# Order of the transfers behind an attention unit, and of three small steps at the start, in a two-layer kernel on one core

## The chip, the cores and the metric

The kernel runs on one core of one Trainium2 chip, in float32. A core has TensorE (PE), VectorE (DVE), ScalarE (ACT), GpSimd (POOL) and SyncE (SP), each with its own instruction stream, and 16 DMA engines that serve transfers issued by SP, ACT and POOL. The metric is the device time of one execution in microseconds (us), as the median of several runs.

## The reference

There are 8 sequences of 128 rows with 512 features. The first layer multiplies each sequence by an adapter matrix chosen by its number (`w0`, 8 matrices of 512x512) and sends the result through a base matrix with eight low-rank experts, of which the top two count. The second layer is attention with a paged cache, then a feed-forward part with 64 small experts. Cut to what matters:

```python
w = weight[adapter_ids];  c = einsum('bsi,boi->bso', x, w)     # adapter matrix by number
x = x + experts(c)                                              # base + top-2 low-rank experts
q, k, v = x Wq, x Wk, x Wv                                      # 32 query heads, 8 key heads, D = 128
q, k = rope(rmsnorm(q)), rope(rmsnorm(k))                       # tables of cos and sin by position
kc, vc = k_cache[block_table], v_cache[block_table]             # 16 pages of 32 rows a sequence
p = softmax(mask([q kc, q k] * SCALE));  o = p [vc; v];  y = o Wo
x = x + ffn(x + y)                                              # 64 experts of rank 8, top 16
```

## The kernel before

**The first layer** is a loop over the 8 sequences (`t`). `l0_load(b)` (L503 to L508) fetches a sequence's `xT` and its adapter matrix (1 MB): SP reads the number from `ids` into a register (`value_load`, L505) and issues the DMAs. For the first sequence the matrix comes in three pieces (256, 256 and 512 KB), all on SP's queue, and PE's first products `cp` (L626) take the pieces one after the other. Until they come PE runs products on an identity matrix whose result nobody uses (L730). Further on in a step, DVE does the routing of the experts (L653 to L671, the last is `low`), PE transposes `low` (`ltp`, L683), and DVE makes the new `x` (L691). Besides, `l0_rows` (L567 to L571) works out, from the page table `vpg`, the row numbers `vrow` by which POOL later gathers value pages, and `l0_angles` (L594 to L607) works out angles for the tables. Both are DVE work put into chosen steps of the loop by hand.

**The attention** is a list of 64 units. A turn `st` is one sequence with one pair of key heads; there are 32 turns, each of two units `u` (`GH = 2`). `iteration(u)` is one pass of a software pipeline written out by hand; its parts work on different units:

- `scores(u, h)` for the four query heads of unit u on PE: against the cached keys `kt` (L439) and the new ones (L442). They need `kt` of the turn and `qkT` of the unit. `mask_exp` follows on DVE (L452) and ACT (L463), `normalize` on DVE and POOL (L468, L469).
- `blocks` (L474) and `blocks_qk` (L425) on DVE transpose 32x32 blocks of the probabilities and of the queries and keys of unit u+2 into `pb`, of which there is one buffer.
- `exchange_out(u)` writes `pb` to DRAM (`px`) in four DMAs of 400 KB, two issued by SP and two by ACT (L486).
- `exchange_in(u - 1)` reads it back in another order: `qkb` (320 KB, queries and keys of unit u+1, L933), then `pT` (1280 KB, probabilities, L936), both issued by SP. `heads_qk` (ACT, L943) copies `qkb` into `qkT`, which the scores of the next unit take. `values(u - 2)` on PE multiplies `pT` with the values (L956).
- `gather` (L193) fetches key pages of the next turn, eight in each unit, 32 KB each: SP reads the page's number into a register and issues the DMA. Five stand ahead of `exchange_in`, three behind it. `gather_v` (L203) on POOL fetches the value pages.
- `make_tables` (L236, POOL) multiplies the norms' weights with cos and sin for a turn, three units ahead.
- `output(u - 3, h)` issues PE's products with the output matrix (`y`, L1081), a head at a time behind the scores of that head; DVE adds them up (L1150, L1168). `project` (L262) makes queries, keys and values for later turns, in blocks of products with sums ahead and behind.

All engines run what was issued in program order. SP's order in a unit is five key pages, `qkb`, `pT`, three key pages, then `px` of the unit:

```python
            if pages:
                gather(st + 1, first, first + 5)
            if on(u - 1):
                exchange_in(u - 1)
            if pages:
                gather(st + 1, first + 5, end)
```

After the last unit PE still has the feed-forward part's tail (L1445).

Of the kernel before, what the change touches and what calls it, by code (L numbers as in the profile page):

```python
# [58 lines left out]
def adaln_ffn_kernel(  # L59
# [374 lines left out]
    def scores(u, h, which=None):  # L434
        st, g = units[u]
        kt, _ = kv_t[st]
        qkT = qkT_t[u]
        s = banks(f"s_{u}_{h}", which)
        nc.tensor.matmul(  # L439
            out=s[:, :L], lhsT=qkT[:, h, :], rhs=kt[:, :, g % GH, :], start=True, stop=True  # L440
        )
        nc.tensor.matmul(  # L442
            out=s[:, L:NK], lhsT=qkT[:, h, :], rhs=qkT[:, REP, :], start=True, stop=True
        )
        s_t[u, h] = s
# [20 lines left out]
    def normalize(u, h):  # L466
        den = den_t.pop((u, h))
        nc.vector.reciprocal(den, den)  # L468
        nc.gpsimd.tensor_scalar(p_t[u, h], p_t[u, h], den, 1.0, ALU.mult, ALU.mult)  # L469
# [23 lines left out]
    with ExitStack() as l0:  # L493
# [6 lines left out]
        def l0_load(b):  # L500
            xT = p2.tile([P, NC, S], F32, tag="xT", name=f"xT_{b}", bufs=3)
            eng = nc.scalar if b == 0 else nc.sync
            eng.dma_start(out=xT.rearrange("p c n -> p (c n)"), in_=xt[b])  # L503
            wt = wt_home.pop(b)
            a = nc.sync.value_load(ids[0:1, b : b + 1])  # L505
            at = (0, P, 2 * P, DM) if b == 0 else (0, DM)
            for n, end in zip(at, at[1:]):
                nc.sync.dma_start(  # L508
                    out=wt.rearrange("p o n -> p (o n)")[:, NC * n : NC * end],
                    in_=w0[ds(a, 1), :, NC * n : NC * end].rearrange("e p n -> p (e n)"),  # L510
                )
            loaded[b] = [xT, wt]

# [77 lines left out]
        def l0_angles(part):  # L591

            if part == 0:
                nc.vector.tensor_copy(lenf, leni)  # L594
                pos = w0p.tile([P, B], F32, name="pos")
                nc.vector.tensor_scalar(pos, lenf, pf, None, ALU.add)
                nc.vector.tensor_tensor(
                    ang,
                    pos.unsqueeze(2).to_broadcast([P, B, D // 2]),
                    fr.unsqueeze(1).to_broadcast([P, B, D // 2]),  # L600
                    ALU.mult,
                )
                nc.vector.tensor_scalar(kk, ang, INV_2PI, ROUND, ALU.mult, ALU.add)
                nc.vector.tensor_scalar(kk, kk, ROUND, None, ALU.subtract)
            elif part == 1:
                for c in (C1, C2, C3):
                    nc.vector.scalar_tensor_tensor(ang, kk, -c, ang, ALU.mult, ALU.add)  # L607
            elif part == 2:
                nc.vector.tensor_scalar(ang, ang, PI_LOW, -PI_LOW, ALU.min, ALU.max)
                nc.vector.scalar_tensor_tensor(kk, ang, -1.0, ang, ALU.mult, ALU.max)  # L610
            else:
                nc.scalar.activation(sin, ang, AF.Sin)
                nc.scalar.activation(cos, kk, AF.Sin, bias=half_pi, scale=-1.0)
# [117 lines left out]
        for t in range(B):  # L731
            l0_adapter(t, True)
            if t >= 1:
                l0_turn_low(t - 1)
            if t == 7:
                scores(0, 1, 1)
                mask_exp(0, 1)
                normalize(0, 0)
            l0_adapter(t, False)
            if t == 0:  # L740
                l0_fold()
            if t + 3 < B:
                l0_load(t + 3)
            if t + 2 < B:
                l0_load_x(t + 2)
            if t in (3, 4):
                load_q(t - 3)
            if 2 <= t <= 5:
                gather(0, (t - 2) * 4, (t - 1) * 4)
            elif t > 5:  # L750
                gather(1, (t - 6) * 8, (t - 5) * 8)
            if t >= 2:
                l0_turn(t - 2)
            if t == 4:
                project_whole(0, 0, 0, 1)
            if t == 5:
                norms(0)
                make_mask(0)
                project_whole(0, 1, 0, 1)
            if t == 6:  # L760
                transpose_qk(0)
                project_whole(0, 0, 1, 1)
            if t == 7:
                make_tables(2)
                norms(2)
                project_whole(0, 1, 1, 1)
                transpose_qk(1)
            if t >= 1:
                l0_experts(t - 1)
            if t == 7:  # L770
                scores(0, 2, 1)
                mask_exp(0, 2)
                normalize(0, 1)
                new_pb(0)
                blocks(0, 0)
            l0_base(t)
            if t == 0:
                l0_small()
            if t == 1:
                l0_rows()  # L780
                nc.vector.tensor_scalar_mul(nw[:, 0, :], nw[:, 0, :], -SCALE)
            if 1 <= t <= 4:
                l0_angles(t - 1)
            if t in (3, 6):
                gather_v(t // 3 - 1, 0, LC)
            if t in (4, 5):
                make_tables(t - 4)
            if t == 4:
                project_whole(0, 0, 0, 0)
            if t == 5:  # L790
                project_whole(0, 1, 0, 0)
                norms(1)
                rotate(0)
                sums_q(nc.gpsimd, 0, 3, 2)
            if t == 6:
                scores(0, 0, 1)
                mask_exp(0, 0)
                project_whole(0, 0, 1, 0)
                rotate(1)
                sums_q(nc.gpsimd, 0, 4)  # L800
            if t == 7:
                scores(0, 3, 1)
                mask_exp(0, 3)
                normalize(0, 2)
                blocks(0, 1)
                project_whole(0, 1, 1, 0, "kv")
# [118 lines left out]
    with ExitStack() as l1:  # L925
# [1 line left out]
        wk2 = l1.enter_context(tc.tile_pool(name="l1_2", bufs=2))  # L927

        def exchange_in(u):
            m = px_t.pop(u).rearrange("k b i f -> (k b) i f")  # L930
            if u + 2 in range(4, NU):
                qkb = wk1.tile([P, QD, NH * 32], F32, tag="qkb", name=f"qkb_{u + 2}")
                nc.sync.dma_start(out=qkb, in_=m[:, :, PW:])  # L933
                qkb_t[u + 2] = qkb
            pT = wk1.tile([P, QD, PW], F32, tag=f"pT{u % 2}", name=f"pT_{u}")
            nc.sync.dma_start(out=pT, in_=m[:, :, :PW])  # L936
            pT_t[u] = pT
# [325 lines left out]
        def iteration(u):  # L1263
# [23 lines left out]
                exchange_in(u - 1)  # L1287
            if pages:
                gather(st + 1, first + 5, end)
            if pages:  # L1290
                gather_v(st + 1, u % GH * LC // GH, (u % GH + 1) * LC // GH)
            if on(u + 3) and u % GH == 1 and u > 1:
                make_tables(units[u + 3][0])
            if on(u - 3) and u % 4 == 3 and (u - 3) // 4 < WHOLE_PAIRS:
                load_y((u - 3) // 4)
# [15 lines left out]
                norms(u + 3)  # L1311
            for h in range(REP):
                if on(u):
                    if (u, h) not in ((1, 0), (1, 1), (2, 0)):
                        scores(u, h)
                        mask_exp(u, h)
                    if h > 0 and (u, h) != (1, 1):
                        normalize(u, h - 1)

                    if (u, h) == (1, 2):  # L1320
                        transpose_qk(3)

                    sums_o(u, h)
                    sums_w(u, h)
                    if 16 <= u < NU - 8 and (r, h) == (2, 3):
                        load_o(u // 16, (1, B12))

                    if h == 2:
                        new_pb(u)
                        if u + 2 in range(4, NU):  # L1330
                            blocks_qk(u + 2, u)
                    if h > 1:
                        blocks(u, h - 2)
                    if h == 1 and u == NU - 5:
                        f_fold()
                    if h == 3:
                        z_blocks(u - NU + 4)
                    if h == (1 if u == NU - 3 else 2) and fb is not None:
                        yT_t[fb] = f_turn(fb, *f)
                if on(u - 3):  # L1340
                    output(u - 3, h)
                    sums_a(u - 3, h)
                if h > 0 and slots:
                    project(k, j, slots[h - 1 : h])

                if (u, h) in WHOLE:
                    project_whole(1, *WHOLE[u, h])
# [12 lines left out]
                f_weights(u - NU + 7)  # L1360
            if on(u):
                normalize(u, REP - 1)
            if 3 < u < NU - 3:
                norms(u + 3)
            if u == 1:
# [192 lines left out]
```

## Time and profile before

| | |
|---|---|
| time, three runs | 1205.39, 1205.78, 1211.27 us; median 1205.78 |
| profiled execution | 1209.55 us, its span 1207.8 us, granted TensorE clock 1.0 |
| PE, DVE, POOL, ACT busy | 99%, 76%, 61%, 42% of the span |
| moved by DMA | 302 MB, 250 GB/s in the mean |
| DMA queues (share of 16 engines) | SP's q1 53.2%, ACT's q10 13.6%, POOL's q0 12.4% |
| one unit of the attention | 16.24 us from px issue to px issue (mean, units 5 to 57) |

In the groups, a row gives line, engine, operation, output and inputs by the program's names with shapes, the number of instructions, busy time and the mean of one in ns, and then the idle time of the engine just ahead of them with what ended it. In the chain of waits a row is the start, the length, and what the time went to, followed back from the last instruction.

### The profile page before, as it was taken

To read this page: it belongs to the slowest core of one execution; us is meant where nothing else is said; L and a number is where in the kernel's file an instruction comes from. 1 tells how busy PE (TensorE), PEld (TensorE's weight loads), DVE (VectorE), ACT (ScalarE), POOL (GpSimd) and SP (SyncE) were. 2 spreads that over 40 slices of the span, in tenths; PEclk is the share of its full clock that TensorE was granted. 3 is DMA by queue.
4 is the path that set the end of the run, shared out by engine and by line. 5 is a ranking of instruction groups with operands and counts; after the bars stand their busy time and mean duration, and the time that the engine had idled before them with its cause. 6 is when DMAs were issued, how large, how long until landed. Compare 5 with 4: busy or idle time off the path is not lost.

```text
span 1207.8 us, 16783 instructions
## 1 busy us (share of the span) xinstructions
PE 1194.7 (99%) x4156; PEld 714.6 (59%) x4156; DVE 913.1 (76%) x2103; ACT 504.3 (42%) x1457; POOL 740.4 (61%) x828
## 2 busy tenths in 40 slices
PE   9999999999999999999999999999999999999998
PEld 7666545565555556555556555555656555555554
DVE  2647788787888787878887887879887888787632
ACT  1345534443444444444444444444444444443211
POOL 3545769778755686578647685687657784643100
PEclk9999999999999999999999999999999999999999
DMA  8823777888888988888789978887989888898742
GB/s 315 287 89 113 247 238 245 263 265 264 264 253 257 301 244 278 260 287 282 237 258 282 294 240 281 285 289 246 279 255 302 254 263 251 261 281 230 232 140 97
DMA packets 205300, 302.31 MB, mean 250 GB/s; under 512 B 84755, under 2 KB 119316, under 8 KB 204180
## 3 DMA queue, kind: packets, MB, share of 16 engines
q1 hardware_dynamic: 170308, 196.81, 53.2%
q10 hardware_dynamic: 18576, 52.04, 13.6%
q0 software_dynamic: 16320, 52.40, 12.4%
q8 instruction: 33, 0.54, 0.2%
q14 instruction: 63, 0.52, 0.1%
HBM read 185.44 MB, written 115.74 MB: 249 GB/s over the span
## 4 chain that ended last, share of the span: by engine, by line
PE 82%; DMA 6%; POOL 4%; DVE 3%; issue 2%; SPq 1%; ACT 1%; ACTq 0%; DVEq 0%; POOLq 0%
PE o L956 18%; PE p L262 18%; PE s L439 16%; PE y L1081 13%; PE s L442 4%; PE p L295 3%; DMA px<-pb 2%; PE op L1445 2%; PE y L1094 2%; PE bp L648 1%; PE cp L626 1%; DMA kt<-in_kc 1%; PE fr L866 1%; POOL p L469 1%; DVE pb L474 1%
## 5 line engine op out<-in xcount | busy, mean ns | idle before, releaser
L463 ACT ACTIVATE p<-p,low 128x640 f32<-128x640 f32 x256 | 211.8, 828 | 433.7 <-DVE den L468 267.4
L469 POOL TENSOR_SCALAR p<-p,den 128x640 f32<-128x640 f32 x256 | 210.2, 822 | 233.4 <-DVE den L468 232.5
L452 DVE CUSTOM_DVE_ANT_0 p<-s,mask,rs 128x640 f32<-128x640 f32 x256 | 222.3, 878 | 81.6 <-PE s L442 80.7
L262 PE MATMUL p<-wqkv,xo 128*128 128x384 f32 x784 | 281.1, 487 | 0.7 <-DVE c L265 0.3
L439 PE MATMUL s<-kt,qkT 128*128 128x512 f32 x504 | 258.7, 595 | 4.5 <-DMA kt<-in_kc 2.6
L956 PE MATMUL o<-pT,vt 128*128 128x512 f32 x512 | 230.2, 592 | 0.0
L474 DVE STREAM_TRANSPOSE pb<-p 128x640 f32<-128x640 f32 x248 | 204.8, 826 | 25.6 <-POOL p L469 25.5
L1081 PE MATMUL y<-wo,oT 128*128 128x256 f32 x784 | 206.6, 380 | 0.9 <-DVE yp L1168 0.5
L262 PEld LDWEIGHTS p<-wqkv,xo 128*128 128x128 f32 x784 | 148.2, 190 | 70.2 <-POOL wqkv L163 1.6
L442 PEld LDWEIGHTS s<-qkT 128*128 128x128 f32 x504 | 95.8, 190 | 120.5 <-issue 120.5
L203 POOL DMA_INDIRECT vt<-in_vc,vrow x128 | 137.6, 1075 | 40.8 <-issue 31.9
L956 PEld LDWEIGHTS o<-pT,vt 128*128 128x128 f32 x512 | 97.2, 190 | 107.8 <-issue 92.8
L439 PEld LDWEIGHTS s<-kt,qkT 128*128 128x128 f32 x504 | 94.2, 190 | 78.3 <-issue 32.5
L1081 PEld LDWEIGHTS y<-wo,oT 128*128 128x128 f32 x784 | 131.9, 191 | 9.8 <-PE s L442 1.2
L311 ACT ACTIVATE sq<-c 128x128 f32<-128x128 f32 x320 | 98.8, 309 | 9.5 <-DVE oT L474 1.4
L442 PE MATMUL s<-qkT 128*128 128x128 f32 x504 | 96.8, 274 | 0.0
L317 POOL TENSOR_TENSOR rs<-ss,mhalf 128x5 f32<-128x5 f32 x64 | 82.2, 1284 | 5.3
L979 ACT COPY oT<-o 128x512 f32<-128x512 f32 x64 | 37.4, 585 | 102.3 <-PE o L956 77.2
L315 POOL TENSOR_SCALAR ss<-ss,eps 128x5 f32<-128x5 f32 x64 | 27.6, 431 | 74.3 <-ACT sq L311 74.3
L956 PE MATMUL o<-pT,vn 128*128 128x512 f32 x128 | 65.4, 592 | 0.0
L425 DVE STREAM_TRANSPOSE pb<-ca 128x640 f32<-128x640 f32 x60 | 50.2, 836 | 18.1 <-DMA px<-pb 8.2
L265 DVE TENSOR_TENSOR c<-c,p 128x384 f32<-128x384 f32 x84 | 44.9, 534 | 22.9 <-PE p L262 22.7
(198 smaller groups left out, 1441.3 us busy)
## 6 DMA issues: line engine op xcount, KB each, us to landing
pT<-px SPq DMA_DIRECT2D x64, 1280.0 KB, 6.6
px<-pb SPq DMA_DIRECT2D x120, 400.0 KB, 5.2
px<-pb ACTq DMA_DIRECT2D x120, 400.0 KB, 4.2
qkb<-px SPq DMA_DIRECT2D x60, 320.0 KB, 3.4
kt<-in_kc SPq DMA_DIRECT2D x512, 32.0 KB, 5.1
wqkv<-in_wqkv POOLq DMA_DIRECT2D x32, 384.0 KB, 4.8
wo<-in_wo POOLq DMA_DIRECT2D x17, 512.0 KB, 7.5
yd<-yp POOLq DMA_DIRECT2D x12, 512.0 KB, 9.0
```

What stands on the lines that cost most here:

```text
L203: nc.gpsimd.indirect_dma_start(out=kv_t[step][1][:, c, :], out_offset=None, in_=vc, in_offset=bass.IndirectOffsetOnAxis(ap=vrow[:, hf, at ...
L262: nc.tensor.matmul(out=ps, lhsT=xo[:, pr, x, c, :], rhs=w[:, c, :], start=(c == 0), stop=(c == 1))
L311: nc.scalar.activation(sq, cs[:, at : at + D], AF.Square, accum_out=ss[:, h : h + 1])
L317: nc.gpsimd.tensor_tensor(rs, ss, mhalf, ALU.pow)
L439: nc.tensor.matmul(out=s[:, :L], lhsT=qkT[:, h, :], rhs=kt[:, :, g % GH, :], start=True, stop=True)
L442: nc.tensor.matmul(out=s[:, L:NK], lhsT=qkT[:, h, :], rhs=qkT[:, REP, :], start=True, stop=True)
L452: nc.vector.tensor_tensor_reduce(out=p, in0=s_t.pop((u, h))[:, :NK], in1=mask_t[st], scale=rs_t[u][:, h : h + 1], scalar=BIG, op0=ALU.add, ...
L463: nc.scalar.activation(p, p, AF.Exp, bias=low, scale=-1.0, accum_out=den)
L469: nc.gpsimd.tensor_scalar(p_t[u, h], p_t[u, h], den, 1.0, ALU.mult, ALU.mult)
L474: nc.vector.transpose(pb_t[u][:, :, h * w : (h + 1) * w].rearrange("p i (j a) -> p j i a", a=32), p_t.pop((u, h)).rearrange("p (j i a) -> ...
L956: nc.tensor.matmul(out=o, lhsT=vt[:, c, j * D : (j + 1) * D] if c < LC else vn_t.pop(u), rhs=pT[:, c], start=(c == 0), stop=(c == LC),)
L1081: nc.tensor.matmul(out=y_t["y"][:, half * HN : (half + 1) * HN], lhsT=part(key)[:, i * S : (i + 1) * S], rhs=wo_t[:, slot(w, key[0] // (B ...
```

## The change

Five places change.

1. The first adapter matrix is fetched in four pieces of 256 KB, issued by SP and ACT in turns. Both engines read the adapter's number into a register of their own.
2. `l0_rows` and the scaling of `nw` move from step 1, ahead of that step's angles, to step 2, behind its angles.
3. `exchange_in` issues only `qkb`. The read of `pT` becomes a function of its own, `probs_in`, called behind the last three key pages of the unit. SP's order becomes five pages, `qkb`, three pages, `pT`, `px`.
4. The tables of turn 3 are made at the end of unit 2, behind its last `normalize`, where unit 3 made them behind its gathers.
5. From unit 5 on, in each fourth unit (u % 4 == 1), the scores of query heads 0 and 1 are both issued ahead of the output products of head 0; before, the scores of head 1 stood behind them.

```diff
@@ l0_load
-            a = nc.sync.value_load(ids[0:1, b : b + 1])
-            at = (0, P, 2 * P, DM) if b == 0 else (0, DM)
-            for n, end in zip(at, at[1:]):
-                nc.sync.dma_start(
+            both = (nc.sync, nc.scalar) if b == 0 else (nc.sync,)
+            which = [e.value_load(ids[0:1, b : b + 1]) for e in both]
+            at = range(0, DM + 1, P if b == 0 else DM)
+            for i, (n, end) in enumerate(zip(at, at[1:])):
+                both[i % len(both)].dma_start(
                     out=wt.rearrange("p o n -> p (o n)")[:, NC * n : NC * end],
-                    in_=w0[ds(a, 1), :, NC * n : NC * end].rearrange("e p n -> p (e n)"),
+                    in_=w0[ds(which[i % len(both)], 1), :, NC * n : NC * end].rearrange("e p n -> p (e n)"),
                 )
@@ first layer, step t
-            if t == 1:
+            if 1 <= t <= 4:
+                l0_angles(t - 1)
+            if t == 2:
                 l0_rows()
                 nc.vector.tensor_scalar_mul(nw[:, 0, :], nw[:, 0, :], -SCALE)
-            if 1 <= t <= 4:
-                l0_angles(t - 1)
@@ exchange_in
-            m = px_t.pop(u).rearrange("k b i f -> (k b) i f")
+            m = px_t[u].rearrange("k b i f -> (k b) i f")
...
+        def probs_in(u):
+            m = px_t.pop(u).rearrange("k b i f -> (k b) i f")
             pT = wk1.tile([P, QD, PW], F32, tag=f"pT{u % 2}", name=f"pT_{u}")
             nc.sync.dma_start(out=pT, in_=m[:, :, :PW])
@@ iteration
                 gather(st + 1, first + 5, end)
+            if on(u - 1):
+                probs_in(u - 1)
             if pages:
                 gather_v(st + 1, u % GH * LC // GH, (u % GH + 1) * LC // GH)
-            if on(u + 3) and u % GH == 1 and u > 1:
+            if on(u + 3) and u % GH == 1 and u > 3:
                 make_tables(units[u + 3][0])
...
-                    if (u, h) not in ((1, 0), (1, 1), (2, 0)):
-                        scores(u, h)
-                        mask_exp(u, h)
+                    ahead = u > 1 and u % 4 == 1
+                    for n in (((0, 1), (), (2,), (3,)) if ahead else ((0,), (1,), (2,), (3,)))[h]:
+                        if (u, n) not in ((1, 0), (1, 1), (2, 0)):
+                            scores(u, n)
+                            mask_exp(u, n)
...
                 normalize(u, REP - 1)
+            if u == 2:
+                make_tables(3)
```

## The prediction

> **What bounds the kernel now.** First the busy table of the page and its row of slices:
>
> ```profile
> PE 1194.7 (99%) x4156; PEld 714.6 (59%) x4156; DVE 913.1 (76%) x2103; ACT 504.3 (42%) x1457; POOL 740.4 (61%) x828
> DMA  8823777888888988888789978887989888898742
> ```
>
> TensorE (PE) is busy for 99% of 1207.8 us. The change takes no matmul away, so all it can give is time in which PE waits. I measured that from the trace's matmul starts: each gap between two starts, less the usual pitch of a matmul of that width (0.84 ns a column). The pitches sum to 1179.0, the gaps to 23.9, the rest is the first start (1.4) and the tail (3.6). These 23.9 us are the pool for any gain; a loss has no such limit. The second row says what else is full: the 16 DMA engines are 0.7 to 0.9 busy from start to end.
>
> Second, the PE groups with what ended the idle time before them, over the span and (last line) over the first 45 us:
>
> ```profile
> L439 PE MATMUL s<-kt,qkT 128*128 128x512 f32 x504 | 258.7, 595 | 4.5 <-DMA kt<-in_kc 2.6 <-ACT oT L979 0.7 <-PE o L956 0.6
> L1081 PE MATMUL y<-wo,oT 128*128 128x256 f32 x784 | 206.6, 380 | 0.9 <-DVE yp L1168 0.5 <-DVE yp L1150 0.4
> L626 PE MATMUL cp<-xT,wqkv 128*128 128x128 f32 x128 | 15.9, 277 | 1.3 <-DMA wqkv<-in_w 1.2
> ...
> L683 PE MATMUL ltp<-ident,low 128*128 128x128 f32 x3 | 0.9, 292 | 0.9 <-DVE low L671 0.9
> ```
>
> These are four of the change's five places: scores that wait for key pages, output products that wait for an addition on VectorE (DVE), the first adapter products that wait for their matrix, and a transpose at 38 us that waits for DVE.
>
> Third, the chain of waits (start, length, what) for the places where DMA sets the pace:
>
> ```profile
> 3.73 5.76 DMA wqkv<-in_w
> ...
> 144.67 5.57 DMA px<-pb
> 156.76 5.78 DMA kt<-in_kc
> ...
> 552.96 7.72 DMA px<-pb
> 567.90 8.62 DMA px<-pb
> 580.70 5.18 DMA kt<-in_kc
> ```
>
> Twice px (the probabilities on their way out) is on the chain as well as the pages: DMA is close behind PE.
>
> **Part 1, first adapter matrix.** In the timeline SP issues the three pieces at 2.62, 3.20 and 3.73 (256, 256, 512 KB). PE starts at 6.03, gaps of 0.26 and 1.37 follow, and the last `cp_0` product ends near 11.5. After: pieces 0 and 2 on SP, 1 and 3 on ACT, which must first read the adapter number (0.47 on SP at 1.94). The pieces share 16 engines that were 0.7 to 0.95 busy under one queue between 3 and 8 us. So two pieces land together, the first later (I estimate 6.4 to 6.9 against 5.9), the last at 8 to 9 against 9.45, as the last 512 KB are cut in two and issued sooner. `cp_0` then ends between 10 and 12. Bounds -1.4 to +0.5 us; I take -0.8, nearer to the gain because the 1.37 gap is the larger one and the last piece ends it. ACT's two issues (some 0.35 each by SP's rows) lie in its wait for the first copy at 11.63; its table load (1.28, from 1.15) is pushed back and still ends by 5. From 12.5 to 37 PE has no gap, so the gain is passed on.
>
> The Trainium skill speaks against this part: its page "DMA: Bandwidth & Descriptors", section "Issuing engines are not separate DMA queues", says that DMAs of different issuers run on the same 16 engines and that a second issuer saves only the time to start one, usually small. By it the gain would be the issue times alone (0.34 and less), with the first piece later: about nothing.
>
> **Part 2, row numbers.** DVE sits at L568 from 27.08 to 30.24 for the page table (`vpg`); then come the rows (0.8), the scaling of `nw` (0.2), and the angles (1.6), so that `x_1` (L691) starts at 33.16, 2 us after its PSUM bank was ready. The routing chain behind ends with `low` at 38.13, and PE waits 1.07 for it. Moved behind the next angles, the wait is over long before; DVE comes 2 us earlier, which is more than 1.07. In its new place the 1.1 us fall into DVE's wait for the third `x` (40.2 to 41.6); without that cover they would cost 1.1. `vrow` has its first reader one step later. -1.07.
>
> **Part 3, key pages ahead of the probabilities.** In each unit SP waits for px, issues qkb (320 KB), pT (1280 KB), then the three last pages. The three pages go into the queue behind 1.28 MB. The scores of each even unit need them:
>
> ```profile
> 577.27 0.54 SPq L933 DMA_DIRECT2D qkb<-px  x1
> 577.86 0.62 SPq L936 DMA_DIRECT2D pT<-px  x1
> 579.01 2.02 SPq L193 DMA_DIRECT2D kt<-in_kc  x3
> ```
>
> In this unit (30) the last page is issued at about 580.7 and lands 5.18 later (the chain above); PE starts the scores 1.21 late. The same kind of gap stands at units 4 (1.76), 14 (0.38), 18 (0.83), 24 (0.17) and 58 (0.59): 4.9 in all. After, the pages are issued 0.6 us sooner and behind 320 KB instead of 1600; pT's packets take about 4 us, so they land 4 to 5 us sooner, and none of these gaps is over 1.8. Next after the pages is `qkT` (ACT L943, ready 1.4 to 7 us before the scores), whose qkb read keeps its place. -4.9, bounds -4.9 to -2.5 (if `qkT` or the mask takes half).
>
> What it delays is pT. Mean over units 2 to 59: px issue to its last packet 8.06, then 0.94 to qkb's issue, then 7.25 to pT's last packet: 16.25, against a unit of 16.24. The ring of transfers is as long as the unit. After, SP issues pT behind three pages (0.84 each), 2.5 later; the pages' own packets then lie ahead of pT, in time that pT used. I put its end 1.95 us later. Values that read pT come 14 us later and do not care. But pT's end now overlaps the next px (first packet 0.8 after its issue; margin before about 0.7), so up to 1.25 us of px wait for shared engines. Who waits for px: qkb, and DVE's L425, as `pb` has one buffer:
>
> ```profile
>   DMA px<-pb: 8.2, 11
>   DMA kt<-in_kc: 6.3, 8
> ```
>
> (idle time of DVE ahead of L425, and how often.) From L425 to the next px issue DVE needs 6.7, px 8.06, release 0.38: 15.1 of 16.24, so 1.1 us a unit are free. Up to 1.1 of the 1.25 is covered; and the engines idle about 2.4 us a unit, which the delayed packets can fill. If all of it fills, no lateness piles up: 0. If the uncovered 0.15 piled up over 56 units: +8.4. I take +0.8, nearer to the filled case, since the clean units keep 1.4 to 1.8 of margin.
>
> **Part 4, tables of turn 3.** On POOL two multiplications (0.73 each) move ahead of two gathers, which come 1.5 later; their readers are a unit away. 0 (±0.3).
>
> **Part 5, two scores ahead** (in the diff alone). In 14 units (u%4=1) both first score pairs stand ahead of the first output products on PE. Those waited twice for an addition of DVE (1.18 us): 0.63 at 306 (unit 13) and 0.58 at 568 (unit 29). The second score pair is 1.4 us of other work in that place, so both gaps go: -1.2. No work is added; the score bank of the second pair is free earlier only if DVE's L452 keeps up, otherwise half of it comes back: -1.2 to 0. I take -1.0.
>
> **Sum.** -0.8 - 1.07 - 4.9 + 0.8 + 0 - 1.0 = -7.0; I leave 0.7 for the next-latest inputs behind those removed (small gaps of 0.4 stand at 180, 545, 1078 and 1144): -6.3. The profiled execution took 1209.55 (span 1207.8, 1.75 around it), 3.8 over the median 1205.78 of the three runs; the same gaps should stand in both, so 1205.8 - 6.3 = 1199.5.
>
> **Rivals.**
> A. The ring closes; slower. px, qkb, pages and pT need more than a unit, each px starts a little later than the last, DVE's L425 and then PE follow. Place: pT's last packets against the next px. It decides when the overlap costs px more than 1.1 us. For: the mean ring is already 16.25 of 16.24 and px stands on the chain. Against: 2.4 us of idle engines. Price: 0.3 us over the free 1.1 in 56 units is +17, less the other gains of 3 and the pages' 4.9: 1205.8 + 17 - 7.8 = 1215; at 0.15 it is even.
> B. The gain is taken by the next wait. Pages come early, but `qkT`, the mask or a late DVE ends last at these six turns, so 4.9 gives 2 and the start 0.3: 1205.8 - 2 - 0.3 - 1.07 - 0.5 = 1202, within 0.5%.
> C. The two queues only delay the first piece and the ring costs the +3 that px's lateness would take through DVE: 1205.8 + 0.5 - 1.07 - 2.5 - 0.5 + 3 = 1205, no change. The change does what it says in all of these; the order of instructions leaves no doubt on that.
>
> **How the numbers follow.** A measurement of this kernel can tell about 0.5%, 6.0 us, from no change: faster is below 1199.75, slower above 1211.8. The forecast with its own spread (1195 to 1203) has 0.56, of which 0.45 lies below 1199.75 and 0.11 above; it reaches low because the small gaps may also go. B has 0.10 and C 0.08 (same); A has 0.26, most of it (0.24) beyond 1211.8. Faster 0.45, same 0.31, slower 0.24. The range takes in B and C and the nearer half of A: 1195 to 1215.
>
> **What would show it.** Right: PE's idle time ahead of L439 falls from 4.5 below 2, with no key pages named; no gap of over 0.5 at 38 us; `cp_0` ends before 11; no gap ahead of the output products in units 13 and 29; pT issued 2.5 later and landed 2 later, with the unit still 16.2. Wrong: units of 16.4 or more, L425 waiting for px in most units (over 15 us in all), px's issue-to-landing time up by over 1 us, or the gaps at the turns still there with another name behind them.

## The result, and the profile after

The changed kernel took 1217.99 us (median of 6 runs, 1217.21 to 1220.42) against 1206.33 for the kernel before (6 runs, 1204.79 to 1211.27): a ratio of 1.0092 with a 95% interval of 1.0072 to 1.0113. It is slower by some 11 us; forecast were 1199.5 and a range up to 1215. The profiled execution took 1220.42 with a span of 1218.3, 10.5 longer than before.

The busy table and the DMA row of the slices, after:

```profile
PE 1198.8 (98%) x4156; PEld 715.6 (59%) x4156; DVE 911.5 (75%) x2103; ACT 502.2 (41%) x1457; POOL 739.8 (61%) x828
DMA  8923777778878878788788888887889888778743
```

The same number of matmuls takes 4.1 us more busy time, which no part of the change explains by itself (see the clock, at the end). The other engines do the same work. PE's gaps beyond its usual pitch, measured as in the prediction, went from 23.9 to 34.5 us: that is the whole difference of the spans.

The group of the projection products (L262) before, and then the PE groups after, the last one over the first 45 us:

```profile
L262 PE MATMUL p<-wqkv,xo 128*128 128x384 f32 x784 | 281.1, 487 | 0.7 <-DVE c L265 0.3 <-POOL wqkv L163 0.3
```

```profile
L262 PE MATMUL p<-wqkv,xo 128*128 128x384 f32 x784 | 283.4, 489 | 10.1 <-DVE c L265 5.9 <-POOL wqkv L163 4.2
L439 PE MATMUL s<-kt,qkT 128*128 128x512 f32 x504 | 259.0, 595 | 3.1 <-DVE low L452 2.7
L1085 PE MATMUL y<-wo,oT 128*128 128x256 f32 x784 | 204.3, 380 | 0.9 <-DVE yp L1172 0.6
...
L627 PE MATMUL cp<-xT,wqkv 128*128 128x128 f32 x128 | 15.3, 276 | 0.8 <-DMA wqkv<-in_w 0.8
```

The key pages are gone from the idle time ahead of the scores (L439), as forecast. In their place the projection products (L262) wait 10.1 us, before 0.7, for sums on DVE and POOL. DVE's group at L425, after and with its releasers, shows what is late on DVE:

```profile
  DMA px<-pb: 32.4, 25
  DMA kt<-in_kc: 20.6, 10
```

Before, these two were 8.2 and 6.3. In the chain of waits of the changed kernel the longest piece is now a px:

```profile
405.38 11.63 DMA px<-pb
```

It can be followed in the timeline (SP and DVE, start and length):

```profile
402.47 0.52 SPq L940 DMA_DIRECT2D pT<-px  x1
404.99 0.82 SPq L486 DMA_DIRECT2D px<-pb  x2
...
417.13 0.84 DVE L425 STREAM_TRANSPOSE pb<-ca 128x640 f32<-128x640 f32 x1 [3.83 <-DMA px<-pb]
417.90 0.80 DVE L474 STREAM_TRANSPOSE pb<-p 128x640 f32<-128x640 f32 x1
418.62 0.52 DVE L265 TENSOR_TENSOR c<-u,p 128x384 f32<-128x384 f32 x1
```

pT is issued only 2.5 us ahead of px; px's last packet then comes 11.4 us after its issue where 8 are usual. DVE stands still for 3.83 at L425, and the sum L265, queued behind it, reaches PE late: in the matmul starts there is a gap of 1.67 at 417.2, between two products of L262.

The mean over units 2 to 58, from the issues and the packets of both traces (px issue is X, qkb issue is c):

| | before | after |
|---|---|---|
| first px packet | X + 0.88 | X + 1.83 |
| last px packet | X + 8.05 | X + 8.55 |
| pT issued | c + 0.63 | c + 3.25 |
| pT's last packet | c + 7.25 | c + 9.53 |
| margin: from that to the next px's X + 0.83, about where px's packets began before | 0.81 | -1.57 |
| units in which the margin is negative, of 57 | 14 | 53 |
| DVE's wait ahead of L425 | 0.30 | 0.93 |

### The profile page after: what moved, and what is told of

It reads as the page before. It is cut to its first block, busy times and chain, and to the rows that moved or that the text cites. A ratio compares the mean times of both kernels' runs of the same rounds, so it can differ in the third digit from the quotient of the medians.

```text
span 1218.3 us, 16849 instructions
## 1 busy us (share of the span) xinstructions
PE 1198.8 (98%) x4156; PEld 715.6 (59%) x4156; DVE 911.5 (75%) x2103; ACT 502.2 (41%) x1457; POOL 739.8 (61%) x828
## 4 chain that ended last, share of the span: by engine, by line
PE 69%; POOL 8%; DMA 8%; DVE 4%; issue 4%; SPq 4%; ACT 2%; ACTq 0%; DVEq 0%; POOLq 0%
PE o L960 16%; PE p L262 14%; PE s L439 12%; PE y L1085 9%; DMA px<-pb 5%; PE s L442 3%; PE p L295 3%; POOL p L469 2%; PE cp L627 2%; PE op L1455 2%; PE bp L649 2%; SPq L192 2%; PE y L1098 2%; DVE pb L474 2%; POOL wqkv L163 1%
## 5 line engine op out<-in xcount | busy, mean ns | idle before, releaser
L262 PE MATMUL p<-wqkv,xo 128*128 128x384 f32 x784 | 283.4, 489 | 10.1 <-DVE c L265 5.9
L439 PE MATMUL s<-kt,qkT 128*128 128x512 f32 x504 | 259.0, 595 | 3.1 <-DVE low L452 2.7
L262 PEld LDWEIGHTS p<-wqkv,xo 128*128 128x128 f32 x784 | 147.7, 190 | 82.3 <-DVE c L265 10.0
L1085 PEld LDWEIGHTS y<-wo,oT 128*128 128x128 f32 x784 | 132.8, 191 | 10.5 <-PE s L442 0.7
L439 PEld LDWEIGHTS s<-kt,qkT 128*128 128x128 f32 x504 | 93.5, 190 | 75.0 <-issue 28.2
L425 DVE STREAM_TRANSPOSE pb<-ca 128x640 f32<-128x640 f32 x60 | 50.4, 840 | 56.4 <-DMA px<-pb 32.4
L315 POOL TENSOR_SCALAR ss<-ss,eps 128x5 f32<-128x5 f32 x64 | 24.9, 388 | 75.0 <-ACT sq L311 75.0
L1154 DVE TENSOR_TENSOR yp<-yp,y 128x512 f32<-128x512 f32 (+3 forms) x94 | 60.1, 639 | 0.0
```

The source lines that it names most:

```text
L262: nc.tensor.matmul(out=ps, lhsT=xo[:, pr, x, c, :], rhs=w[:, c, :], start=(c == 0), stop=(c == 1))
L439: nc.tensor.matmul(out=s[:, :L], lhsT=qkT[:, h, :], rhs=kt[:, :, g % GH, :], start=True, stop=True)
L1085: nc.tensor.matmul(out=y_t["y"][:, half * HN : (half + 1) * HN], lhsT=part(key)[:, i * S : (i + 1) * S], rhs=wo_t[:, slot(w, key[0] // (B ...
```

## The experiments

Three theories stood at the start. R: the ring of transfers; pT's later end runs into the next px, DVE waits at L425 and PE behind it. S: the new order of scores (part 5) costs. E: the earlier start shifts the first units against the DMA traffic. "Parts" are those of the change. Ratios are to the kernel before, run on the same chip, with a 95% interval.

**All but part 3.**

```diff
             if on(u - 1):
                 exchange_in(u - 1)
+                probs_in(u - 1)
             if pages:
                 gather(st + 1, first + 5, end)
-            if on(u - 1):
-                probs_in(u - 1)
```

> All of the change but its third part: pT is read ahead of the last three key pages again. Theory R (the ring of transfers: pT's end runs into the next px, which makes DVE's L425 late and through it PE): the loss goes and the gains of the start stay, 1203.0 to 1205.5, with L425 waiting 15 us or less for DMA in all, as before. Theory S (the order of scores, part 5, costs): 1212 or more, as the third part has little to do with it. Theory E (the early start only shifts the first units against the DMA traffic, and PE's lost clock at 156 us costs the rest): 1208 or more, with the clock drop at 156 us still there.

1205.17 us, ratio 0.9993 (0.9975 to 1.0012). The loss is gone.

**Part 3 alone.** The kernel before with `probs_in` behind the last pages.

> The kernel before with the third part alone. Theory R: it carries the loss, 1216 to 1221, with L425 waiting 40 us or more for DMA and the gaps of PE at L262. Theory S: 1206 or less (the key-page gaps of 4.9 us gone, nothing lost). Theory E: 1201 to 1206, no clock drop at 156 us.

1222.31 us, ratio 1.0144 (1.0124 to 1.0165). It is 15 us slower than the kernel before (1207.35 in these runs): a little more than R expected, and more than the whole change loses. The four executions lie between 1215.80 and 1225.07, and the profile is of the fastest. In it DVE's L425 waits 53.0 us in all, and PE's projection products wait 5.1 and its output products 5.1:

```profile
  DMA px<-pb: 36.4, 26
  DMA kt<-in_kc: 12.7, 5
...
L262 PE MATMUL p<-wqkv,xo 128*128 128x384 f32 x784 | 283.0, 488 | 5.1 <-DVE c L265 4.0 <-POOL wqkv L163 1.0
L1084 PE MATMUL y<-wo,oT 128*128 128x256 f32 x784 | 206.8, 380 | 5.1 <-DVE yp L1153 3.3 <-DVE yp L1171 1.4 <-POOL ss L315 0.2
```

S and E fall.

**All but part 5.**

```diff
-                    ahead = u > 1 and u % 4 == 1
+                    ahead = False
```

> The whole change without its fifth part (scores of head 1 behind the output products again). Theory R: within 2 us of the changed kernel, 1216 to 1220. Theory S: the loss goes, 1200 to 1208.

1217.49 us, ratio 1.0098 (1.0082 to 1.0114): the same as the whole change. Part 5 neither costs nor gives anything that shows in the time. At its own place it does what was meant: by the two profiles PE idles 3.3 us ahead of the output products without it and 0.9 with it. But ahead of the projection products it idles 5.1 without it and 10.1 with it, so the wait seems only to move.

**Parts 1 and 2 alone.**

> The kernel before with the first two parts alone. Theory R: faster by the 1.8 us by which the changed kernel's PE was ahead at 98 us, 1203.5 to 1205.5; a part may be lost again in the first units. Theory E: 1207 or more, with the gap at 152 us and the lower clock behind it.

1204.92 us, ratio 0.9984 (0.9972 to 0.9997). No version measured here is faster. By the ratio it gains 1.9 us on the kernel before.

**Where part 3 costs: without the weights' loads.** Both kernels leave out the loads of the projection weights in the attention, so that later products use old weights:

```diff
                     for n, i in LOADS_Q[r]:
-                        load_q(group + n, i)
+                        wq_t[group + n] = wq_t[group + n - GH]
```

> The kernel before, leaving out the loads of the projection weights (384 KB each, 24 of them, in units 7 to 12, 23 to 28 and 39 to 44), so that later products use old weights. Within 1% of the kernel before: 1199 to 1207, as TensorE's work is the same and the transfers were mostly hidden.

> The kernel before with part 3 alone, again without those loads. With them part 3 cost 15 us. Theory R, contended units (pT's delay does harm where the loads of weights fill the idle time of the 16 engines, and is absorbed elsewhere): at most 5 us over the same kernel without part 3. Rival (the ring is too long in every unit, loads or not): 10 to 17 us over it.

1204.90 us, ratio 0.9989 (0.9971 to 1.0006), without part 3; 1206.67, ratio 1.0000 (0.9981 to 1.0020), with it. Part 3 costs 1.8 us here and 15 with the loads. pT still ends late (c + 9.47 in the mean, a margin of -1.51), but DVE's wait at L425 is 25.9 in all, less than half of the 53.0 with the loads. Its group in the kernel with part 3 and no loads:

```profile
L425 DVE STREAM_TRANSPOSE pb<-ca x60: 818/836/846, 138.0 to 1096.2; 128x640 f32<-128x640 f32 x60
its engine sat idle before it (us, times) until:
  DMA px<-pb: 18.2, 17
  DMA kt<-in_kc: 4.5, 3
```

The four traces say where the time goes. The table sums the time from each px issue to the next, and DVE's wait ahead of L425, over the 18 units that load projection weights and over the other 41 of units 2 to 60:

| us | before | part 3 alone | no loads | no loads, part 3 |
|---|---|---|---|---|
| 18 units with loads | 296.2 | 305.8 | 292.4 | 292.2 |
| the other 41 units | 664.8 | 662.6 | 666.5 | 665.7 |
| L425's wait, 18 units | 5.1 | 28.7 | 0.2 | 1.7 |
| L425's wait, other 41 | 13.0 | 24.4 | 12.2 | 24.1 |

In the 41 units part 3 doubles L425's wait and the units get no longer: what the lateness costs there is no more than the gaps of the key pages gave, some 5 us in all. What part 3 loses on balance in its profile, it loses in the 18. There, with part 3 alone, the DMA engines are 0.98 busy in the first 9 us after px's issue and px's last packet is at X + 9.10 (before, 0.87 and X + 7.92); with part 3 and no loads they are 0.90 busy and it is at X + 8.03. So the overlap by itself does not set most of the price; what else has to be done in that unit does. Without the loads GpSimd is also spared the issuing (some 0.79 us for each of the 24), and how much of the price goes by its time was not separated.

Busy DMA engines alone do not tell. Around the 3.83 wait, in a unit in which POOL's queue loads a weight of the output product, they are full in the changed kernel, but in the same windows of the kernel before, where L425 waits 0.28, they are full as well (before first; the last two columns are DMA share and GB/s):

```profile
404.00:410.00 6.00, 6.00 (x23) 3.86 (x22) 4.89 (x12) 2.00 (x4) 5.31 (x8) 1.00 1.00 318
410.00:416.00 6.00, 6.00 (x24) 3.91 (x24) 3.97 (x10) 1.85 (x6) 2.19 (x3) 1.00 1.00 324
...
404.00:410.00 6.00, 6.00 (x22) 3.68 (x21) 4.38 (x9) 2.97 (x13) 3.37 (x5) 1.00 0.94 307
410.00:416.00 6.00, 6.00 (x23) 3.87 (x22) 2.48 (x8) 3.02 (x7) 4.87 (x7) 1.00 1.04 396
```

**pT behind one page instead of three** (with parts 1 and 2):

```diff
             if pages:
-                gather(st + 1, first + 5, end)
+                gather(st + 1, first + 5, first + 6)
+            if on(u - 1):
+                probs_in(u - 1)
+            if pages:
+                gather(st + 1, first + 6, end)
```

> The kernel before with parts 1 and 2, and with pT read behind one of the three last pages instead of none (the kernel before) or all three (the change). pT is issued 0.84 us later in place of 2.6. Theory R as a margin: pT's end had 0.8 to 0.9 us before the next px's packets, so 0.84 nearly uses it up and little is lost: 1203 to 1208. Rival (each microsecond of delay of pT costs the same): a third of the change's loss, 1209 to 1213.

1213.03 us, ratio 1.0056 (1.0034 to 1.0079): the margin reading missed by 5 us, and the rival's number came out for another reason. L425 waits no more than before (0.22 a unit). What came back, larger, are the key pages. PE's groups in this kernel:

```profile
L262 PE MATMUL p<-wqkv,xo 128*128 128x384 f32 x784 | 280.7, 486 | 0.6 <-DVE c L265 0.6
L439 PE MATMUL s<-kt,qkT 128*128 128x512 f32 x504 | 258.9, 595 | 10.9 <-DMA kt<-in_kc 4.2 <-DMA px<-pb 3.7 <-ACT oT L983 1.0
```

The likely reason is the two pages that are still issued behind pT, as pT now ends at c + 8.38 in place of 7.16; the profile names the key pages for 4.2 us of the wait and px for 3.7. By the matmul starts the turns' gaps are 12.8 us against 1.9 with parts 1 and 2 alone: 10.9 more, against 8.1 more in the time.

**The pages issued by ScalarE** (with parts 1 and 2): `gather(st + 1, first + 5, end, nc.scalar)`, pT right behind qkb.

> The kernel before with parts 1 and 2, and with the three last pages of each unit issued by ScalarE (same place in program order) in place of SyncE; pT stays right behind qkb. Theory R: the pages no longer stand behind 1.28 MB, the key-page gaps of 4 to 5 us go, pT is not later and the ring is not longer: 1198 to 1203. Rival (what costs is three small transfers and their register loads in any place of the ring, and ScalarE's time): 1207 or more.

1241.97 us, ratio 1.0312 (1.0274 to 1.0351). R's number missed by 40 us, not through a late pT (its last packet is at c + 7.03) but through ScalarE. Its timeline in one unit, with the page issues ahead of its copy of `oT`:

```profile
599.88 0.86 ACTq L486 DMA_DIRECT2D px<-pb  x2
601.87 5.71 ACTq L193 DMA_DIRECT2D kt<-in_kc  x3
607.62 0.58 ACT L980 COPY oT<-o 128x512 f32<-128x512 f32 x1 [8.57 <-DMA kt<-in_kc]
```

Three page issues take 5.7 us of its queue here. Of the idle time ahead of L980, 149.3 us in 23 units are put down to the pages and 178.9 in 27 to px, whose issues stand in the same queue; before, neither is named there.

**pT in two halves, one on each side of the pages** (with parts 1 and 2):

```diff
-            nc.sync.dma_start(out=pT, in_=m[:, :, :PW])
+            nc.sync.dma_start(out=pT[:, : QD // 2], in_=m[:, : QD // 2, :PW])
...
+        def probs_in(u):
+            pT, m = pT_t[u]
+            nc.sync.dma_start(out=pT[:, QD // 2 :], in_=m[:, QD // 2 :, :PW])
```

> The kernel before with parts 1 and 2, and with pT read in two DMAs of 640 KB: the first right behind qkb, the second behind the three last pages. In the runs so far pT's last packet came 6.3 to 6.9 us after its issue wherever it stood, so a half should take about 3.3: first half done at qkb's issue + 4, pages landed by + 5 to 6 (before, + 7 and more), second half issued at + 3.9 and done at + 7.2 to 7.6, as before (7.2). Theory R: the key-page gaps go and pT is not later, 1199 to 1203. Rival (any transfer issued behind the pages reaches into the next px): pT ends at + 8.5 or later and the time is 1207 to 1213.

1204.94 us, ratio 0.9987 (0.9969 to 1.0006): by time between the two readings, and by mechanism half of each. No turn waits for pages, as R had it. But pT is later, as the rival had it: the second half is issued at c + 3.89, its last packet comes 4.65 after that, and so pT ends at c + 8.54 in place of 7.16 with parts 1 and 2 alone. The margin to the next px is -0.57 in the mean and negative in 39 of 57 units. The time is that of parts 1 and 2 alone. There the pages' gaps were only 1.9 us in its profile, so little was left to win, and this much overlap costs little. PE's groups with the halves:

```profile
L262 PE MATMUL p<-wqkv,xo 128*128 128x384 f32 x784 | 281.2, 487 | 1.1 <-DVE c L265 1.1
L439 PE MATMUL s<-kt,qkT 128*128 128x512 f32 x504 | 258.0, 593 | 2.1 <-DVE low L452 2.0
...
L1087 PE MATMUL y<-wo,oT 128*128 128x256 f32 x784 | 206.5, 380 | 1.2 <-DVE yp L1156 1.1
```

All three now wait for DVE, whose L425 waits 28.5 us in all (17.1 with parts 1 and 2 alone).

**Sums ahead of the wait.** With parts 1 and 2, DVE's first steps into `pb` are moved behind the sums of the third projection block; once without and once with part 3:

```diff
-                    if h == 2:
-                        new_pb(u)
-                        if u + 2 in range(4, NU):
-                            blocks_qk(u + 2, u)
-                    if h > 1:
+                    if h == 3:
                         blocks(u, h - 2)
...
                 if h > 0 and slots:
                     project(k, j, slots[h - 1 : h])
+                if on(u) and h == 2:
+                    new_pb(u)
+                    if u + 2 in range(4, NU):
+                        blocks_qk(u + 2, u)
+                    blocks(u, 0)
```

> The kernel before with parts 1 and 2, and with DVE's first two steps into pb (L425 and the first L474) put behind the sums of the third projection block of the unit instead of ahead of them. It moves no transfer in SP's order. Theory R: within 2 us of the kernel with parts 1 and 2 alone, 1203 to 1207; the next px can come a little later.

> The same, and part 3 (pT behind the pages). In the changed kernel DVE's wait at L425 held up the sums (c, L265) that PE's projection products wait for. Theory Q (that queue is the way from px to PE): with the sums ahead of the wait most of the 15 us goes, 1201 to 1208, and PE's gaps at L262 fall below 3 us. Theory X (the ring itself sets the unit, whatever is queued behind L425, as px, qkb and the next scores come late): 1215 or more, with the gaps moved to the scores (L439) or L452.

1218.11 us, ratio 1.0082 (1.0059 to 1.0105), and 1220.53, ratio 1.0104 (1.0082 to 1.0126). Both first readings missed: the move alone costs 13 us, and Q falls, since with it and part 3 the time is no better. With the move alone PE waits for the scores' inputs; the turns' gaps are 9.2 us against 1.9 with parts 1 and 2 alone:

```profile
L439 PE MATMUL s<-kt,qkT 128*128 128x512 f32 x504 | 259.1, 596 | 9.5 <-DMA kt<-in_kc 4.6 <-ACT oT L980 2.1 <-DVE low L452 1.6
```

In the kernel with part 3, PE's wait at L262 on DVE's sum is gone, and others stand in its place:

```profile
L262 PE MATMUL p<-wqkv,xo 128*128 128x384 f32 x784 | 281.8, 488 | 2.8 <-POOL wqkv L163 2.8
L439 PE MATMUL s<-kt,qkT 128*128 128x512 f32 x504 | 259.2, 596 | 6.5 <-DVE low L452 6.4
...
L1085 PE MATMUL y<-wo,oT 128*128 128x256 f32 x784 | 207.6, 382 | 8.0 <-DVE yp L1154 4.0 <-DVE yp L1172 2.5 <-POOL ss L315 1.3
```

No one step behind L425 is the way to PE: DVE loses the time, and whatever PE needs from it next comes late. The pair also suggests how little play L425 has. It starts 1.1 us later behind px's landing (2.06 in place of 0.95) with no change in SP's order, and the kernel loses about as much as by part 3; with that in place part 3 adds only 2.4. The move changes DVE's own order too, so this is a sign and no measurement of the play.

## Why the prediction was wrong, step by step

- **Part 1** (-0.8 forecast): right in size between the two profiles. The last `cp_0` product ends at 10.9 in place of 11.6. The shape was as forecast too, with the first product later (7.09 for 6.03) and no gap after it. The size is uncertain, as the start differs between executions. PE's next products start at 11.5 in the kernel before and at 11.1, 12.7 and 12.8 in the three other traces with the old start; in the nine with the new one they start at 10.5 to 11.0. The page "DMA: Bandwidth & Descriptors" of the Trainium skill, section "Issuing engines are not separate DMA queues", gives the saved issue time alone as the gain. The trace fits that: the first product comes 1 us later and the last one sooner, and the 0.7 gained is about two of SP's issues of 0.34.
- **Part 2** (-1.07): right. No gap is left at 38 us. At 98 us PE is 1.81 ahead of before, by the first two parts 1.87 were forecast, and the run with these alone gave 1.9.
- **Part 3, gain** (-4.9): right in place. The turns' gaps went from 5.2 to none, in the changed kernel and in part 3 alone. The size belongs to one execution, which took 3.8 us over the median. With SP's order unchanged the gaps were 5.3 without the loads, 4.2 with all but part 3 and 1.9 with parts 1 and 2 alone, so the prediction's "the same gaps should stand in both" does not hold.
- **Part 3, price** (+0.8 forecast, 0 to 8.4 as bounds): this is the step that failed. Part 3 alone lost 15 us net and gained up to 5 at the turns, so its price was up to 20 by the medians (11 by the two profiles, of which part 3's is a fast one). The inputs were near: pT issued 2.6 later (2.5), ended 2.3 later (1.95), overlap 1.57 (1.25). Two inferences from means were wrong. "The engines idle about 2.4 us a unit, which the delayed packets can fill" comes near the truth in the 41 units without loads, which got no longer; in the 18 with loads it fails, and there part 3 adds 9.6 us by the px issues. "1.1 us a unit are free" was a mean as well: 14 of 57 units already had no margin before, and L425 already waited in 25. A wait that exceeds the play in some units was not paid back by the others, so the price had to be summed over units. The prediction's own chain of waits had px on it three times, where it counted two. Rival A named the place, the waiters and the sign, at 1215 and with a chance of 0.26. Its price, 0.3 us in each of 56 units, came near by luck, as the loss sits in 18 units.
- **Part 4** (0): it has no run of its own; all but part 3 and parts 1 and 2 alone differ by 0.25 us, within the scatter, so parts 4 and 5 together show nothing without part 3.
- **Part 5** (-1.0): wrong, 0 (and the code has 15 such units, where it counted 14). Two gaps ahead of the output products, of 0.75 and 0.46, stand in the changed kernel; undoing the part changes nothing in the time.
- **Sum.** -1.9 for the start, and about +13 for part 3 in the presence of the others (1217.99 less 1205.17), is the +11 measured.

How much of the price is px's own slowness and how much the later qkb behind it was not separated: no kernel with a second `pb` buffer was tried.

## What to carry to other kernels

A transfer that nobody waits for can still set the pace by its end: ask what is issued next, who waits for that, and take the margin unit by unit, in the units with the most other work, not as a mean of the span. A gap read in one execution is that execution's: compare it with others of the same order before counting on it. Where two transfers compete for the place ahead of a deadline, moving all of the large one trades one wait for another; cut in two around the small ones, it brought them in time and ended 1.4 us later, which here cost about what the pages gave. Before moving work off a full queue to another engine, look at what stands behind it in that engine's stream.

## What the runs showed of the hardware that was not expected

**PE's clock can drop after a wait of 2 us.** In the changed kernel PE waited 2.8 us at 152 us and 2.2 at 1085. In both places its trace then has a granted clock of 0.5 for 3.41 us. The windows of the changed kernel (PE busy first, the third number from the end is the granted clock):

```profile
150.00:156.00 6.00, 3.36 (x11) 1.66 (x10) 2.77 (x7) 0.92 (x2) 3.01 (x3) 0.99 0.70 222
156.00:162.00 6.00, 6.00 (x12) 2.77 (x11) 5.78 (x15) 1.54 (x3) 1.60 (x2) 0.72 0.78 264
...
1085.00:1092.00 7.00, 4.99 (x13) 2.93 (x13) 5.51 (x15) 3.12 (x7) 1.60 (x2) 0.76 0.67 208
```

6 us at 0.72 and 7 at 0.76 lose 1.7 us each (6 x 0.28, 7 x 0.24), 3.4 in all: a third of the loss on top of the waits themselves, and most of the 4.1 us of extra busy time. The kernel before, whose longest wait was 1.76 in its trace, has 1.00 at the first of these places. Over all the traces of this case, no wait of PE of up to 2.02 us was followed by such a drop. Of those from 2.13 up, all were but two: 2.24 at 157 us (no loads, part 3) and 2.34 at 11 us (no loads). So the length of the wait does not decide alone. The kernel before is not free of drops in its other executions: in one set of 24, six had a mean clock of 0.995 to 0.998 and took 1208.9 to 1213.2 us, the others 1203.2 to 1210.2. The Trainium skill's page "TensorE: Matmul & The Clock Gate", section "HAM oscillation — how this bites in real kernels", warns of idle gaps over about 3.4 us; here 2.2 and 2.8 were enough, so the measurement says to keep further away from that figure.

**A large read lands about the same time after its issue.** pT's last packet came 6.6 us after its issue right behind qkb, 6.9 behind one page and 6.3 behind three; its place in the queue hardly mattered. That is why moving the issue by 2.6 moved the end by nearly as much. Half the bytes did not take half the time: the second half alone, behind the three pages, took 4.65.
